# A two-layer graph network: ten and eight node tiles by counts instead of nine and seven, layer 2's first rows fetched in layer 1, and pools that wait for their own bytes

## The chip, the core and the metric

One core of one Trainium2 chip runs the whole program. The metric is the device time of one execution in microseconds (us), the median of several runs. The engines are TensorE (PE, matrix products; its weight loads are PEld), VectorE (DVE), ScalarE (ACT), GpSimd (POOL) and SyncE (SP, which only issues DMAs). Each engine runs its own instructions in the order in which they were written.

## The reference

6250 nodes have 256 features each, and 100,000 edges are sorted by `dst`. `dst` is the integer part of 6250 u² for uniform u, so nodes with low numbers receive many more edges than the others. All is fp32.

```
agg = segment_sum(x[src], dst); h = (1+eps1)*x + agg
h = relu(h @ W1a + b1a)          # 256 -> 512
h = relu(h @ W1b + b1b)          # 512 -> 512
agg = segment_sum(h[src], dst); h = (1+eps2)*h + agg
h = relu(h @ W2a + b2a)          # 512 -> 512
out = h @ W2b + b2b              # 512 -> 256
return layernorm(x + out)
```

## The kernel before

The nodes are 49 tiles of 128 (the last has 106 rows). A layer aggregates each tile in one of two ways, and then runs its dense part.

**By gathers.** POOL issues an indirect DMA (line 503) that fetches 128 source rows of the table into a piece of a ring (`early`; in layer 2 also `late`). PE sums the 128 rows into up to 32 nodes with a one-hot matrix (L1177, `bank<-early,sel`, two fp32 matmuls a gather in the trace), a split and merge (ACT L1207, DVE L1212, PE L1222) places the sums, and DVE adds them to the tile's `acc` (L1234). A gather can be issued when a piece of the ring is free, that is, when PE has summed what was in it.

**By counts.** For the "heavy" tiles, those with the lowest numbers and so the most edges, the kernel makes a matrix that says how many edges lead from each source node to each node of the tile. It is counted in layer 1 by products of one-hot factors (PE L1886, `bank<-cb,ca`, factors by DVE L1833 and L1843; ACT L1927 and DVE L1935 copy the counts into `at` and `at_first`). Counts times table then replace the gathers:

- Layer 1 (L1761, `bank<-cf,xh`) takes the heavy tiles in three passes of `PASSED` tiles each. Every pass runs over the 49 row tiles of x, in two fp32r halves kept in DRAM (`halves`), so a matmul is as wide as its pass has tiles times 128 columns: 256, 512 and 384.
- Layer 2 (L1613, `bank<-upper,cf` and `bank<-xr,cf`) runs over 13 ranges of the 49 row tiles, the last range (one tile) first, then ranges of four tiles. For a range, SP loads the rows of h (`xr<-h`, L866) and the saved counts (`ci<-counts`, L1527), ACT and DVE split the rows in two halves (L1503, L1504, L1508), ACT converts the counts (L1540, `cf<-ci`), and for each heavy tile PE multiplies 2 x 4 matmuls into a bank, which ACT (L1551) or DVE (L1556) adds to `acc`.

The number of heavy tiles is `HEAVY` = (9, 7): nine in layer 1, seven in layer 2. All others are gathered: 454 gathers in layer 1, 494 in layer 2 (rows of 512 fp32, twice as long).

The dense part of a tile transposes `acc` (PE L1300, ACT L1321), and multiplies twice (PE L1349, ACT L1359 with relu, PE L1378). In layer 1, DVE L1388 and ACT L1391 finish the tile, and ACT's queue writes it to h (`h<-h1r`, L866). In layer 2, DVE L1400 to L1423 and ACT L1418 make the layernorm. Layer 2's gathers may read any row of h, so its first one waits for layer 1's last write of h.

**What sets the order.** A planner simulates the engines with a cost for each operation when the program is built. Each step is a `yield ("on", engine, cost, priority)`; of the steps that are ready, an engine takes the one with the lowest number. The order that comes out is fixed in the program. Where PE has nothing ready, `filling()` inserts matmuls without a use (L1246, `bank<-numbers`, priority 9). Buffers come from pools `keep`, `loan` and `psum`, opened anew for each layer.

Of the kernel before, what the change touches and what calls it, by code (L numbers as in the profile page):

```python
# [26 lines left out]
HEAVY = (9, 7)  # L27
# [4 lines left out]
RANGE = 4  # L32
PAIR = 2
PASSED = (2, 4, 3)
# [178 lines left out]
def dve(n):  # L213
    return 0.085 + 0.00105 * n


def act(n):
    return 0.12 + 0.00083 * n
# [152 lines left out]
def tile_gin_residual_layernorm(  # L371
# [520 lines left out]
    def ordered(ctx):  # L892
# [20 lines left out]
        halves = odram.tile([N, 2 * D], F32, name="halves")  # L913

        def layer(number, ctx, table, width, scale, wa, ba, wb, bias, wide):
# [17 lines left out]
            class Tiles(Room):  # L933

                def __init__(self, pool, shape, dtype, name, bufs):
                    super().__init__(plan, bufs, False)
                    self.make = lambda: pool.tile(shape, dtype, tag=name, name=name, bufs=bufs)

# [33 lines left out]
            ready = {t: Event(plan) for t in range(NT)}  # L972

# [63 lines left out]
            def scaling(b, token):  # L1037
# [8 lines left out]
                yield ("on", "ACT", act(len(ts) * width), 2)  # L1046
# [208 lines left out]
            def dense(b):  # L1255
# [115 lines left out]
                for i, t in enumerate(ts):  # L1371
# [11 lines left out]
                    def finish(token=token, i=i, t=t, m=m, po=po, todo=todo):  # L1383
                        if once:
# [7 lines left out]
                            in_parts(nc.scalar, h1[t * P : t * P + m, :], h[:m])  # L1392
                            h_token.release()
# [71 lines left out]
            cf_room = Tiles(loan, [P, max(PASSED) * P] if once else [P, RANGE, P], F32R, "cf", 3)  # L1465
# [4 lines left out]
            def second_products():  # L1470
                xr_room = Tiles(loan, [P, RANGE, width], F32R, "xr", 2)
                upper_room = Tiles(loan, [P, RANGE, width], F32R, "upper", 2)
                ci_rooms = [
                    Tiles(
                        loan, [P, RANGE, len(ts) * P], U8 if ts[0] else U16, f"ci{ts[0]}", 2
                    )
                    for ts in kept
                ]
# [8 lines left out]
                def rows_of():  # L1487
                    for r in rs:
# [6 lines left out]
                        upper = upper_token.tile  # L1495
                        halves_of[r] = xr_token, upper_token
                        whole = xr.bitcast(F32)
                        todo = Count(plan)
                        for j, k in enumerate(ks):
                            m = rows(k)  # L1500
                            token = yield ("get", banks, 2)
                            yield ("on", "ACT", 2 * act(width), 3)
                            nc.scalar.copy(upper[:m, j, :], whole[:m, j, :])  # L1503
                            nc.scalar.copy(bank[token.number][:m, :width], whole[:m, j, :])  # L1504

                            def lower(j=j, m=m, token=token):
                                yield ("on", "DVE", dve(width), 3)
                                nc.vector.tensor_tensor(  # L1508
                                    xr[:m, j, :], bank[token.number][:m, :width], upper[:m, j, :],
                                    op=ALU.subtract,  # L1510
                                )
                                token.release()
                                todo.less()

                            todo.more()
                            plan.then(plan.start, lower())
                        yield ("until", todo)
# [117 lines left out]
            def first_products():  # L1635
# [62 lines left out]
                def factoring():  # L1698
                    for n, ts in enumerate(PASSES):
# [9 lines left out]
                        for k in range(NT):  # L1709
# [12 lines left out]
                            if k + 1 in ends:  # L1722
                                plan.start(saving(ts, ranges[ends.index(k + 1)]))
# [517 lines left out]
```

## Time and profile before

| | us |
|---|---|
| median of 3 runs (lowest, highest) | 1544.63 (1540.19, 1547.57) |
| profiled execution | 1555.75 |
| its span from the first to the last instruction | 1553.9 |
| PE busy (share of the span) | 1296.1 (83%) |
| POOL busy | 919.0 (59%) |
| DVE busy | 801.4 (52%) |
| ACT busy | 599.3 (39%) |

The profile is one execution, 11 us longer than the median. Stages, by the names of instructions: until 27 us the lists of edges are prepared, layer 1 runs to its last write of h at about 760 us, the first gather of layer 2 stands at 765.25 and its last at 1514.92. A busy time counts an instruction from start to end; neighbouring matmuls overlap, so the mean duration of a matmul is above the spacing of a dense run of them.

### The profile page before, as it was taken

The numbers are of one execution on the slowest core, as the hardware profiler recorded it, in microseconds if no ns is written. First come the engines' busy times: TensorE is split into PE (matmuls) and PEld (weight loads), VectorE is DVE, ScalarE is ACT, GpSimd is POOL, SyncE is SP. The second block draws the span as 40 slices with busy tenths as digits, with TensorE's granted clock in tenths as the row PEclk, the third lists the DMA queues.
The fourth block names the chain that finished last, engine by engine and source line by source line (L and its number), as shares of the span: only waits on it lengthen the run. The fifth ranks groups of instructions, "written<-read, shape, count | busy, mean of one in ns | idle before, by whom it ended". The sixth has DMA issues, their size and how long they took to land.

```text
span 1553.9 us, 20355 instructions
## 1 busy us (share of the span) xinstructions
PE 1296.1 (83%) x6363; PEld 806.0 (52%) x6363; DVE 801.4 (52%) x2078; ACT 599.3 (39%) x1256; POOL 919.0 (59%) x976
## 2 busy tenths in 40 slices
PE   3478888887888889998878898998989799899866
PEld 2144454444544446654435566665656566566533
DVE  5575666666457762122146666765555454433331
ACT  3655665544554434432433433423332333211111
POOL 7556665556656665663265666665666566566560
PEclk7589999988989999999999999999999999999988
DMA  4554776645865337962588677777787677666661
GB/s 119 160 172 139 234 227 192 219 131 157 252 207 176 113 116 230 293 182 81 175 284 299 206 242 224 263 219 238 240 252 227 214 241 243 186 199 192 190 205 28
DMA packets 156749, 309.63 MB, mean 199 GB/s; under 512 B 35118, under 2 KB 69894, under 8 KB 156632
## 3 DMA queue, kind: packets, MB, share of 16 engines
q0 software_dynamic: 61312, 189.07, 40.3%
q1 hardware_dynamic: 87844, 105.57, 21.0%
q10 hardware_dynamic: 7476, 13.60, 2.4%
q8 instruction: 54, 0.88, 0.2%
q14 instruction: 63, 0.52, 0.1%
HBM read 269.32 MB, written 38.82 MB: 198 GB/s over the span
## 4 chain that ended last, share of the span: by engine, by line
PE 63%; DVE 11%; issue 9%; another core or an unknown queue 7%; ACT 4%; DMA 2%; DVEq 0%; SPq 0%; ACTq 0%
PE bank L1349 16%; PE bank L1378 14%; PE bank L1177 10%; PE bank L1613 7%; PE bank L1761 7%; PE bank L1886 4%; PE bank L1222 3%; DVE acc L1234 3%; PE bank L1300 2%; DMA acc<-h 1%; DVE at L1935 1%; DVE acc L1556 1%; PE bank L1246 1%; DVE split L1212 1%
## 5 line engine op out<-in xcount | busy, mean ns | idle before, releaser
L503 POOL DMA_INDIRECT early<-in_x_dram,srcs x454 | 442.4, 974 | 271.6 <-issue 114.6
L503 POOL DMA_INDIRECT early<-h,srcs x250 | 241.0, 964 | 190.2 <-issue 113.1
L503 POOL DMA_INDIRECT late<-h,srcs x244 | 233.2, 956 | 134.5 <-issue 62.9
L1234 DVE SCALAR_TENSOR_TENSOR acc<-bank,mask,acc 128x256 f32<-128x256 f32 (+1 forms) x369 | 211.6, 611 | 73.4 <-PE bank L1222 27.5
L1177 PE MATMUL bank<-early,sel 128*32 128x256 f32 (+1 forms) x1408 | 166.8, 502 | 42.6 <-issue 24.0
L1378 PE MATMUL bank<-wide_w,ht 128*128 128x512 f32 (+1 forms) x392 | 195.6, 626 | 6.4 <-DVE h1r L1388 3.2
L1349 PE MATMUL bank<-zt,wide_w 128*128 128x256 f32 (+2 forms) x832 | 184.0, 375 | 18.6 <-issue 11.1
L1349 PEld LDWEIGHTS bank<-zt,wide_w 128*128 128x128 f32 x832 | 152.4, 194 | 50.6 <-issue 19.2
L1761 PE MATMUL bank<-cf,xh 128*128 128x256 f32 (+3 forms) x588 | 142.6, 376 | 23.1 <-issue 14.4
L1613 PE MATMUL bank<-upper,cf 128*128 128x512 f32 (+1 forms) x343 | 151.6, 442 | 8.1 <-ACT upper L1503 4.3
L1927 ACT CAST at<-bank 128x441 f32 (+4 forms) x214 | 106.1, 507 | 95.7 <-PE bank L1886 25.7
L1613 PE MATMUL bank<-xr,cf 128*128 128x512 f32 (+1 forms) x343 | 137.9, 402 | 3.0 <-issue 1.3
L1126 DVE TENSOR_TENSOR sel<-iota,slot 128x256 f32<-128x256 f32 (+4 forms) x111 | 48.8, 440 | 164.4 <-PE bank L1177 94.5
L1886 PE MATMUL bank<-cb,ca 128*128 128x490 f16 (+7 forms) x347 | 89.7, 349 | 52.3 <-DVE cb L1843 21.1
L1761 PEld LDWEIGHTS bank<-cf,xh 128*128 128x128 f32 (+1 forms) x588 | 101.0, 198 | 56.1 <-issue 34.3
L1556 DVE TENSOR_TENSOR acc<-bank,acc 128x512 f32<-128x512 f32 x84 | 56.9, 684 | 129.0 <-remote 69.5
L1222 PE MATMUL bank<-split,to 128*128 128x512 f32 (+2 forms) x310 | 90.6, 399 | 39.1 <-ACT split L1207 17.3
L1540 ACT CAST cf<-ci 128x512 fp32r<-128x512 uint8 (+3 forms) x91 | 53.3, 594 | 175.6 <-remote 56.6
L1177 PEld LDWEIGHTS bank<-early,sel 128*32 128x32 f32 x1408 | 40.1, 112 | 148.1 <-issue 124.9
L1349 PE MATMUL bank<-zt,narrow_w 128*128 128x256 f32 (+2 forms) x432 | 105.4, 394 | 11.7 <-ACT zt L1321 8.2
L1843 DVE TENSOR_SCALAR cb<-numbers,spot 128x492 f16<-128x492 f16 (+7 forms) x328 | 94.7, 327 | 36.2 <-PE bank L1886 12.9
L1378 PEld LDWEIGHTS bank<-wide_w,ht 128*128 128x128 f32 (+1 forms) x392 | 73.1, 198 | 77.5 <-issue 64.4
(150 smaller groups left out, 1702.3 us busy)
## 6 DMA issues: line engine op xcount, KB each, us to landing
xh<-halves SPq DMA_DIRECT2D x48, 512.0 KB
h<-h1r ACTq DMA_DIRECT2D x48, 256.0 KB
halves<-xh SPq DMA_DIRECT2D x24, 512.0 KB
xr<-h SPq DMA_DIRECT2D x12, 1024.0 KB
acc<-h SPq DMA_DIRECT2D x19, 512.0 KB
early<-in_x_dram,srcs POOLq DMA_INDIRECT x454
raw<-in_x_dram SPq DMA_DIRECT2D x12, 512.0 KB
r<-in_x_dram SPq DMA_DIRECT2D x22, 256.0 KB
```

Of the source, the lines that this page charges most:

```text
L503: nc.gpsimd.indirect_dma_start(out=rows_[:, j, :], out_offset=None, in_=table, in_offset=bass.IndirectOffsetOnAxis(ap=srcs[:, c : c + 1], ...
L1177: mm = nc.tensor.matmul(pm[b * SLOTS : (b + 1) * SLOTS], sel[:, c - groups[g][0], :], rows_[:, l, :], start=(c == part[0]), stop=(c == par ...
L1222: nc.tensor.matmul(pu[:, i * width : (i + 1) * width], to[:used], split[:used, l, i * width : (i + 1) * width], start=(l == 0), stop=(l == 1),
L1234: nc.vector.scalar_tensor_tensor(acc[t], pu[:, i * width : (i + 1) * width], mask[:, t - lo[g], g : g + 1], acc[t], op0=ALU.mult, op1=ALU.add,
L1349: nc.tensor.matmul(ph[:, (f - o) * TILES * P : (f - o) * TILES * P + nb], wa[:, k, f * P : (f + 1) * P], zt[:, k, :nb], start=(k == 0), st ...
L1378: nc.tensor.matmul(po[:m], ht[:, f, i * P : i * P + m], wb[:, f, :], start=(f == 0), stop=(f == KH - 1),)
L1556: nc.vector.tensor_tensor(acc[t], bank[token.number][:, :width], acc[t], op=ALU.add)
L1613: nc.tensor.matmul(bank[token.number][:, :width], cf[:m, j, :], of[:m, j, :], start=(j == 0 and of is upper), stop=(j == len(ks) - 1 and o ...
L1761: nc.tensor.matmul(to[:, :c], of, factor, start=(k == 0 and l == 0), stop=last, skip_group_check=True,)
L1843: made = nc.vector.tensor_scalar(token.tile[:, :e], numbers[:, :e], spot[:, c : c + 1], None, op0=ALU.is_equal,)
L1886: mm = nc.tensor.matmul(bank[token[l].number][:, : (k1 - k0) * w], a.tile[:, c % BATCH, :], b.tile[:, k0 * w : k1 * w], start=(j == 0), st ...
L1927: nc.scalar.copy(of[:, k0:k1, UNDER - w + 1 :][:, :, bass.ds(v, w - 1)], ap[:, :, : w - 1],)
```

## The change

- `HEAVY` (9, 7) becomes (10, 8) and `PASSED` (2, 4, 3) becomes (2, 4, 4): one more tile by counts in each layer.
- `SOONER` = 2: a new task `sooner()` in layer 1 waits until all counts are saved and the rows of h in question are written, then loads the first two ranges of layer 2 (one tile and four tiles) and halves them with `halving()`, at priority 8, the lowest of real work.
- `at` and `at_first` move into a pool of their own, which is closed in layer 1; the bytes go to a pool `side2` with the buffers `xr`, `upper`, `cfs` and `ci` of layer 2, given out there by the class `Views`.
- The pools `keep`, `loan`, `psum` and `side2` get `reuse_waits="tile"`: a buffer waits for the former users of its own bytes only.
- The counting matmuls go from priority 1 to 0 on PE. The scaling of `acc` on ACT in layer 2 goes from priority 2 to 4.

```diff
-HEAVY = (9, 7)
+HEAVY = (10, 8)
...
+SOONER = 2
 PAIR = 2
-PASSED = (2, 4, 3)
+PASSED = (2, 4, 4)
...
+        def make_views():
+
+            side.close()
+            pool = ctx.enter_context(tc.tile_pool(name="side2", bufs=1, side="right", reuse_waits="tile"))
...
+            some("xr", 2, [RANGE, H], F32R)
+            some("upper", 2, [RANGE, H], F32R)
+            some("cfs", 3, [RANGE, P], F32R)
+            for ts in kept:
+                some(f"ci{ts[0]}_", 2, [RANGE, len(ts) * P], U8 if ts[0] else U16)
...
-            keep = ctx.enter_context(tc.tile_pool(name=f"keep{number}", bufs=1))
-            loan = ctx.enter_context(tc.tile_pool(name=f"loan{number}", bufs=1))
+            keep = ctx.enter_context(tc.tile_pool(name=f"keep{number}", bufs=1, reuse_waits="tile"))
+            loan = ctx.enter_context(tc.tile_pool(name=f"loan{number}", bufs=1, reuse_waits="tile"))
             psum = ctx.enter_context(
-                tc.tile_pool(name=f"psum{number}", bufs=1, space=bass.MemoryType.PSUM)
+                tc.tile_pool(name=f"psum{number}", bufs=1, space=bass.MemoryType.PSUM, reuse_waits="tile")
             )
...
-                yield ("on", "ACT", act(len(ts) * width), 2)
+                yield ("on", "ACT", act(len(ts) * width), 2 if once else 4)
...
+            def halving(ks, xr, upper, width, first, todo):
+
+                whole = xr.bitcast(F32)
+                for j, k in enumerate(ks):
+                    m = rows(k)
+                    token = yield ("get", banks, first - 1)
+                    yield ("on", "ACT", 2 * act(width), first)
+                    nc.scalar.copy(upper[:m, j, :], whole[:m, j, :])
+                    nc.scalar.copy(bank[token.number][:m, :width], whole[:m, j, :])
+
+                    def lower(j=j, m=m, token=token):
+                        yield ("on", "DVE", dve(width), first)
+                        nc.vector.tensor_tensor(
+                            xr[:m, j, :], bank[token.number][:m, :width], upper[:m, j, :],
+                            op=ALU.subtract,
+                        )
+                        token.release()
+                        todo.less()
...
-                    for r in rs:
+                    for i, r in enumerate(rs):
                         ks = ranges[r]
                         xr_token = yield ("get", xr_room, 0)
                         xr = xr_token.tile
-                        in_rows(ks, xr.bitcast(F32), table)
-                        yield ("rest", LOAD + 3.0)
+                        if i >= SOONER:
+                            in_rows(ks, xr.bitcast(F32), table)
+                            yield ("rest", LOAD + 3.0)
...
+                def sooner():
+                    yield ("until", saved)
+                    make_views()
+                    for i, r in enumerate(reversed(range(len(ranges) - SOONER, len(ranges)))):
+                        ks = ranges[r]
+                        for k in ks:
+                            yield ("until", written[k])
+                        xr = views["xr"][i]
+                        in_rows(ks, xr.bitcast(F32), h1[:, :])
+                        yield ("rest", LOAD + 3.0)
+                        yield from halving(ks, xr, views["upper"][i], H, 8, Count(plan))
...
-                        yield ("on", "PE", sum(0.01 + NT * wides[x[1]] / 2400 for x in todo[k : k + 2]), 1)
+                        yield ("on", "PE", sum(0.01 + NT * wides[x[1]] / 2400 for x in todo[k : k + 2]), 0)
```

Lines below the edits move by 34 or so: L1177 before is L1211 in the changed kernel, L1613 is L1648, L1503 and L1504 are L1509 and L1510, L1391 is L1425.

On ACT, the last writes of layer 1 and the first range of layer 2 stood like this before (`h1r` is a finished tile of layer 1, `upper` the upper half of a range's rows, `cf` the converted counts):

```order
L1391 ACTIVATE h1r<-h1r 128x512
L866 DMA h_60<-h1r 128x512
L1047 ACTIVATE acc<-acc,e_93 128x1024 x4
L1540 CAST cf<-ci_7010 128x128
L1503 CAST upper<-xr 106x512
L1504 COPY bank_6972<-xr 106x512
```

In the changed kernel the halving stands among the finishing of layer 1's tiles, at this place on ACT:

```order
L1355 COPY zt<-bank_498 128x2x128
L1509 CAST upper_6770<-xr_6768 128x512
L1510 COPY bank_501<-xr_6768 128x512
L1425 ACTIVATE h1r<-h1r 128x512
L867 DMA h_60<-h1r 128x512
L1509 CAST upper_6770<-xr_6768 128x512
L1510 COPY bank_502<-xr_6768 128x512
L1425 ACTIVATE h1r<-h1r 128x512
L867 DMA h_60<-h1r 128x512
```

All five row tiles of the first two ranges are halved there, and ACT's layer 2 starts with conversions of counts.

On PE, the first sums of gathered rows of layer 2 stood before in the midst of the second range, here ahead of its fourth heavy tile (24 of its 56 matmuls are ahead of the sums):

```order
L1613 MATMUL bank_6972<-upper,cf 128x512
L1613 MATMUL bank_6972<-xr,cf 128x512
L1177 MATMUL bank_6974<-early,sel_7034 32x512 x2
L1177 MATMUL bank_6975<-early,sel_7034 32x512 x4
L1177 MATMUL bank_6976<-early,sel_7043 32x512 x4
L1613 MATMUL bank_6977<-upper,cf 128x512
```

In the changed kernel they stand behind all products of both ranges, and what follows (`upper_6769`) is the third range:

```order
L1648 MATMUL bank_7133<-upper_6770,cfs_6771 128x512
L1648 MATMUL bank_7133<-xr_6768,cfs_6771 128x512
L1211 MATMUL bank_7128<-early,sel_7180 32x512 x2
L1211 MATMUL bank_7134<-early,sel_7180 32x512 x4
L1211 MATMUL bank_7129<-early,sel_7193 32x512 x4
L1648 MATMUL bank_7130<-upper_6769,cfs_6772 128x512
```

So 80 product matmuls (16 of the one-tile range, 64 of the next) are ahead of the first sum, where 38 were.

Near the end of PE's order, the last product of layer 2 before had 100 of the 494 gathers' sums behind it:

```order
L1613 MATMUL bank_6972<-upper,cf 128x512
L1613 MATMUL bank_6972<-xr,cf 128x512
L1177 MATMUL bank_6974<-late,sel 32x512 x12
L1300 MATMUL bank_6973<-ident,acc 128x128 x4
L1300 MATMUL bank_6976<-ident,acc 128x128 x4
```

In the changed kernel the last product stands among the last tiles' dense parts:

```order
L1648 MATMUL bank_7129<-upper_6769,cfs_6772 128x512
L1648 MATMUL bank_7129<-xr_6767,cfs_6772 128x512
L1256 MATMUL bank_7133<-split,to 128x512 x2
L1383 MATMUL bank_7130<-zt,wide_w 128x128 x8
L1334 MATMUL bank_7134<-ident,acc 128x128 x4
L1383 MATMUL bank_7128<-zt,wide_w 128x128 x8
L1211 MATMUL bank_7132<-early,sel 32x512 x8
```

Of 474 sums 20 are left behind it. By counts of the orders, the changed kernel has 442 and 474 gathers (12 and 20 fewer), 98 more products in layer 2, 24 more counting matmuls, 196 products of layer 1 with 512 instead of 384 columns, and 42 matmuls of L1246 instead of 98. Behind layer 1's last sum PE has 16 first and 8 second dense matmuls before, and 32 and 20 in the changed kernel (the trace shows each of these fp32 matmuls as two).

## Rows read from the trace of the kernel before

**Rows 1.** The page: busy time of each engine, share of the span, instructions.

```profile
PE 1296.1 (83%) x6363; PEld 806.0 (52%) x6363; DVE 801.4 (52%) x2078; ACT 599.3 (39%) x1256; POOL 919.0 (59%) x976
```

**Rows 2.** Windows by stage: from:to, length, each engine's busy us, clock, DMA share, GB/s.

```profile
120.00:720.00 600.00, 508.05 (x2572) 299.13 (x2565) 327.66 (x901) 286.88 (x639) 370.94 (x381) 0.93 0.61 189
720.00:760.00 40.00, 37.52 (x172) 19.93 (x171) 6.79 (x13) 10.03 (x25) 0.00 (x0) 0.96 0.28 87
760.00:800.00 40.00, 27.68 (x89) 12.93 (x87) 9.08 (x18) 19.92 (x40) 23.39 (x25) 0.83 0.79 276
800.00:1470.00 670.00, 600.39 (x2937) 407.33 (x2936) 363.34 (x721) 212.62 (x415) 421.81 (x440) 0.98 0.73 229
1470.00:1554.00 84.00, 57.58 (x307) 31.73 (x305) 22.41 (x55) 10.23 (x25) 28.94 (x31) 0.85 0.41 120
```

**Rows 3.** Windows of POOL's gathers (L503) alone: busy us and number, clock, DMA.

```profile
27.00:720.00 693.00, 425.66 (x438) 0.89 0.60 185
765.00:1516.00 751.00, 474.14 (x494) 0.96 0.73 230
```

**Rows 4.** Waits of POOL, 120 to 720 us: releaser, us in total, times, longest.

```profile
POOL early L503 <- PE bank L1177: 47.3, 20, 5.3
POOL early L503 <- PE bank L1886: 45.0, 22, 5.3
```

**Rows 5.** Waits of POOL, 800 to 1480 us.

```profile
POOL late L503 <- PE bank L1177: 44.2, 11, 10.4
POOL early L503 <- PE bank L1177: 32.5, 7, 7.3
```

**Rows 6.** Groups of PE by shape: count, busy us, mean ns, idle before.

```profile
L1761 PE MATMUL bank<-cf,xh 128*128 128x512 f32 x192 | 59.6, 442 | 14.4 <-issue 10.7 <-ACT cf L1719 3.7
L1761 PE MATMUL bank<-cf,xh 128*128 128x384 f32 x192 | 46.9, 374 | 6.3 <-ACT cf L1719 4.6 <-issue 1.7
L1886 PE MATMUL bank<-cb,ca 128*128 128x275 f16 x19 | 7.2, 383 | 18.5 <-DVE cb L1843 15.5 <-DVE at L1935 1.7 <-DVE acc L1234 1.2
```

**Rows 7.** Pieces of the chain that ended last: start us, us, what.

```profile
514.66 0.60 PE bank L1886 x4
...
1231.14 1.85 PE bank L1613 x8
...
1456.78 2.71 PE bank L1177 x24
```

**Rows 8.** Windows of PE's L1246 alone (clock and DMA are the stage's).

```profile
705.00:760.00 55.00, 7.03 (x21) 1.96 (x22) 0.94 0.31 97
760.00:800.00 40.00, 7.96 (x27) 2.45 (x24) 0.83 0.79 276
1470.00:1554.00 84.00, 15.55 (x48) 4.42 (x48) 0.85 0.41 120
```

**Rows 9.** Timeline of PE at layer 1's end, behind its last sum.

```profile
747.94 3.84 PE L1349 MATMUL bank<-zt,narrow_w 128*128 128x128 f32 x32
751.61 7.03 PE L1378 MATMUL bank<-wide_w,ht 128*128 128x512 f32 x16
```

**Rows 10.** Timeline at layer 2's start: start us, us, instruction, [idle before <-releaser].

```profile
765.60 0.80 PE L1613 MATMUL bank<-upper,cf 106*128 106x512 f32 x1 [4.34 <-ACT upper L1503]
...
778.11 0.50 PE L1613 MATMUL bank<-upper,cf 128*128 128x512 f32 x1 [2.05 <-issue]
...
783.89 0.63 PE L1613 MATMUL bank<-xr,cf 128*128 128x512 f32 x1
784.32 0.61 PE L1613 MATMUL bank<-upper,cf 128*128 128x512 f32 x1
```

**Rows 11.** The chain at layer 2's end.

```profile
1504.30 14.39 another core or an unknown queue
1518.70 0.59 ACT split L1207
...
1538.67 0.67 PE bank L1300 x4
```

More of the change, by code (lines that the diff above doesn't have):

```diff
@@ L913, in ordered, with some @@
         halves = odram.tile([N, 2 * D], F32, name="halves")
+        side = ExitStack()
+        sides = side.enter_context(tc.tile_pool(name="side1", bufs=1, side="right"))
+        at = sides.tile([P, NT, -(-(HEAVY[0] * P + UNDER - BASE) // 4) * 4], U8, name="at")
+        at_first = sides.tile([P, NT, P + UNDER + UNDER % 2], U16, name="at_first")
+        views = {}
+        def make_views():
+            side.close()
+            pool = ctx.enter_context(tc.tile_pool(name="side2", bufs=1, side="right", reuse_waits="tile"))
+            def some(name, count, shape, dtype):
+                views[name] = [
+                    pool.tile([P] + shape, dtype, name=f"{name}{i}") for i in range(count)
+                ]
+            some("xr", 2, [RANGE, H], F32R)
[3 more added lines that the diff above has]
+                some(f"ci{ts[0]}_", 2, [RANGE, len(ts) * P], U8 if ts[0] else U16)
         def layer(number, ctx, table, width, scale, wa, ba, wb, bias, wide):
@@ L937, in __init__, with take @@
                     self.make = lambda: pool.tile(shape, dtype, tag=name, name=name, bufs=bufs)
+            class Views(Room):
+                def __init__(self, views):
+                    super().__init__(plan, len(views), False)
+                    self.views = views
+                def take(self):
+                    token = super().take()
+                    token.tile = self.views[token.number]
+                    return token
             def reach(g):
@@ L972, in layer @@
             ready = {t: Event(plan) for t in range(NT)}
+            written = {t: Event(plan) for t in range(NT)}
             def settle(t):
@@ L1392, in finish @@
                             in_parts(nc.scalar, h1[t * P : t * P + m, :], h[:m])
+                            plan.then(written[t].set)
                             h_token.release()
@@ L1463, in beside_rows @@
                 return some
-            cf_room = Tiles(loan, [P, max(PASSED) * P] if once else [P, RANGE, P], F32R, "cf", 3)
+            cf_room = Tiles(loan, [P, max(PASSED) * P], F32R, "cf", 3) if once else Views(views["cfs"])
+            def halving(ks, xr, upper, width, first, todo):
[14 more added lines that the diff above has]
+                        todo.less()
+                    todo.more()
+                    plan.then(plan.start, lower())
             if once:
@@ L1491, in rows_of @@
                         xr = xr_token.tile
-                        in_rows(ks, xr.bitcast(F32), table)
-                        yield ("rest", LOAD + 3.0)
+                        if i >= SOONER:
+                            in_rows(ks, xr.bitcast(F32), table)
+                            yield ("rest", LOAD + 3.0)
                         upper_token = yield ("get", upper_room, 0)
-                        upper = upper_token.tile
                         halves_of[r] = xr_token, upper_token
[L1497 to L1517, printed above, removed]
+                        if i >= SOONER:
+                            todo = Count(plan)
+                            yield from halving(ks, xr, upper_token.tile, width, 3, todo)
+                            yield ("until", todo)
                         plan.then(halved[r].set)
@@ L1736, in saving @@
                             )
+                    saved.less()
                 def multiplying():
```

15 lines of the change are left out of this document (5 added, 10 removed).

## The prediction

> **What bounds the kernel now.** I read the page's busy times first, then the windows by stage, because a share over the whole span mixes stages with different limits. PE is the busiest engine, 1296.1 us of 1553.9, and POOL is far from full [rows 1]. By stage, PE is busy 508 of 600 us in layer 1's main part (density 0.847) and 600 of 670 in layer 2's (0.896), POOL only 371 and 422 [rows 2]. The gathers, on which POOL spends 0.96 us each, follow each other at a slower pace: 693 us for 438 is 1.58 us in layer 1, 751 us for 494 is 1.52 in layer 2 [rows 3]. So POOL itself doesn't set the pace. What it waits for is PE: in layer 1, 47.3 us end with sums and 45.0 with counting matmuls [rows 4] (POOL's idle time there is 600 - 371 = 229 us), in layer 2, 76.7 us with sums [rows 5]. POOL waits for a free piece of the ring, the piece waits for its sum, and the sum waits for its turn in PE's fixed order. Neither PE nor the gathers bound alone: PE's order holds the gathers back, and gathers not yet landed leave PE idle.
>
> Three stretches are worse than this steady state:
> - The end of layer 1 (720 to 760): POOL does nothing, since layer 2's gathers need all of h; PE is busy 37.5 of 40 us, but from 705 on 7.0 us of that are matmuls of L1246, which do nothing useful [rows 2, 8].
> - The start of layer 2 (760 to 800): PE is busy 27.7 us, 8.0 of them L1246, so 20.3 us of 40 are lost [rows 2, 8]. Its first product waited 4.34 us for ACT to halve rows, and the second range came 12.5 us later, after another gap [rows 10].
> - The end of layer 2 (1470 to 1554): of 84 us PE is busy 57.6, and 15.6 of these are L1246, so 42 us are lost [rows 2, 8]. The products are over by then, and the chain stands 14.4 us on something in flight before the last merge [rows 11]; the last gather was issued at 1514.92.
>
> **Layer 1, part by part.** PE gets more work. The 196 matmuls of the third pass become 512 wide: the 384-wide ones take 374 ns and the 512-wide ones 442, 68 ns more, so at most 13.3 us; by the spacing in a dense run, a matmul of 512 takes 1.85/8 = 0.23 us [rows 7], a quarter of it 0.058, so 11.3 [rows 6]. I take 12. The 24 counting matmuls cost 24 x 0.15 = 3.6 us in a dense run [rows 7] and 24 x 0.383 = 9.2 at their full duration [rows 6]; I take 6. The eight more of the small products with the identity and two merges fewer are about nothing, within 1 us either way. Twelve gathers fewer save PE about 2 us: half as wide as layer 2's, whose sums take 2.71/12 = 0.226 us a gather [rows 7], they cost between half of that and all of it, 1.4 to 2.7. Sum: +16 us of PE. The copies of the counts on ACT and DVE (24 each) lie beside: ACT is busy 287 and DVE 328 of 600 us [rows 2]; if that cover were gone, they would add their own durations, by the nearest row 24 x 0.38 = 9 us [rows 6].
>
> The gathers get shorter: 12 x 1.58 = 19 us. But more dense work is behind the last sum: 64 and 40 matmuls of the trace instead of 32 and 16, so at 3.84/32 and 7.03/16 us each [rows 9] 25.3 us instead of 10.9, +14. With a few us of L1246 and waits that stood in this tail replaced, I take +11. So if gathers lead, layer 1 changes by -19 + 11 = -8. If PE leads, it is +16, less about 10 us for the L1246 matmuls and gaps of the end that the dense work now fills: +6. If nothing is filled it is +16. The rows speak for both: of POOL's 229 us idle 92 are for PE [rows 4], the rest are not. I take the middle of the first two, **-1 us**, and keep -8 and +16 as bounds. Moving the counting to priority 0 on PE is in this: it frees counts earlier and makes sums wait; 45 us of POOL's waits already end with counting matmuls [rows 4], so it can cost as well as gain, and I give it no term.
>
> **Layer 2's start.** The first two ranges are halved during layer 1. On ACT and DVE that is ten copies and five subtractions in a stretch where both are mostly idle (10.0 and 6.8 of 40 us) [rows 2], ahead of some of the last writes of h; there it could delay the first gather by the copies that stand in front of the last write, one pair or two, which the range holds. At the start PE then has 80 products ready as soon as counts are there, 42 more than stood ahead of the first sum before. At 0.23 us they are 9.7 us of work in a stretch where 20 us were lost. The sums behind them don't come later for it, since their rows had not landed by then. I take **-8 us**; bounds 0 (the counts land too late as well, or the first landings decide) and -12 (the whole gap to the second range).
>
> **Layer 2's middle.** 98 products more x 0.23 = +22.6 us, 20 gathers' sums fewer x 2.71/12 = 0.226 are -4.5 [rows 7], two merges fewer -1: +17 us of PE. At the stage's density of 0.896 that is 17/0.896 = **+19 us**. The other bound is the gathers' side, 20 x 1.52 = -30 us.
>
> **Layer 2's end.** Products now reach almost to the last sum (20 sums behind the last product instead of 100), so the 42 us lost at the end have work to fill them. The last tile's way from its last gathered row to the output can't be filled: from 1538.67, where the last transpose starts [rows 11], it is 15.2 us to the end of the span. That leaves 42 - 15 = **-27 us** at best for PE; lower bound -10, where only the matmuls of L1246 are replaced in part and the wait for the last landings stays.
>
> **The sum.** -1 - 8 + 19 - 27 = -17 us. Against the profiled execution of 1555.75 this gives about 1539, and since that execution lies 11 us above the median, 1544.63 - 17, about **1527 us** by the median. That pools wait for their own bytes alone and the scaling of `acc` has gone to priority 4 is costed at nothing beside this: before, ACT's scalings stood ahead of the first halving, which is now in layer 1; the start's bounds hold it.
>
> **Clock.** PE's granted clock shows in the rows: 0.83 in 760 to 800 and 0.85 in the last 84 us, against 0.98 in the middle [rows 2]; two neighbouring products at the start are 0.43 us apart [rows 10], against 0.23 in the dense run. So after idle time PE runs at the lower of its two levels, 1.2 GHz, for a while. The change leaves out 56 of 98 matmuls of L1246. The Trainium skill ("TensorE: Matmul & The Clock Gate", section "HAM oscillation — how this bites in real kernels") says that PE which waits for data falls back to the cold clock and starts the next burst cold, which speaks against leaving them out. The trace agrees that the clock is lower where PE waits.
>
> **Rivals.**
> - *PE is the bound and the end doesn't give back* (slower). The end's gap may belong to the last gathers' landing, not to the order [rows 11], and PE at 0.896 may take no more. Then layer 1 costs +16, the middle +19, the start gives -8, the end -10: +17, about 1562 us. For it: 33 us of PE added and the longest wait at the end has POOL's last gathers in it. Against: the end's 100 sums without a product beside them. It decides where the last product still comes long before the end, or density in the middle stays under 0.90.
> - *Gathers set the pace throughout* (much faster). Layer 1 -8, start -8, middle and end -30, the tail as before: -46, about 1499 us. For it: the constant pace [rows 3]. Against: POOL's waits end with PE [rows 4, 5], and PE has more to do.
> - *Nothing comes of the fetch in layer 1, and gains and work cancel*: the start 0 because the saved counts and the first gathers' landing decide as before, layer 1 +2, middle +19, end -20: +1, about 1545.
> - *The clock falls* where L1246 is missing: the start and the end at 0.5 instead of 0.84 would take 28 + 42 us of work 0.84/0.5 = 1.7 times as long, at most +47; as products take the place of most L1246 matmuls, I price it at +18 on the forecast, again 1545.
>
> **Chances.** Forecast 0.45 (its own range 1515 to 1537), PE as the bound 0.24, gathers as the pace 0.16, cancelling 0.10, clock 0.05. A measurement of this kernel can tell about 0.5%, 8 us, from no change: faster (under 1537) 0.45 + 0.16 = 0.61, same 0.15, slower 0.24. The range reaches from 1497 (half of the gather case is left out, 0.08) to 1560 (half of the PE case, 0.12).
>
> **What would show it.** Right: in the 40 us after layer 1's last write PE has over 34 us of useful work; the stretch from layer 1's last sum to its last write grows to some 25 us, and that write comes at 759 +- 10; products run to within 40 us of the end, the L1246 matmuls there are few, and the lost time of the last 84 us is under 20. Wrong: layer 1's last write after 770 (counting at priority 0 starves the sums, POOL's waits on L1886's successor grow), a gap of PE in the first 40 us of layer 2 as long as before (counts not there), gathers at 1.6 us and more in layer 2, or the same wait of 14 us before the last merge.

## The result, and the profile after

The changed kernel takes 1526.76 us (median of 4 runs, 1519.56 to 1538.76); the kernel before, run beside it, 1546.1 us. The ratio is 0.989, with a 95% interval from 0.9847 to 0.9934: faster, by about 1.1%. 1527 us were predicted. The profiled execution took 1526.32 us with a span of 1524.6; that of before took 1555.75 us, 10 us above its median, so the two profiles differ by 29 us where the medians differ by 19. Below, differences between the two profiles are told as such.

Windows of the changed kernel by stage, with the columns of [rows 2]; its layer 1 ends at 745.52, so the stages are shifted:

```profile
690.00:745.00 55.00, 54.66 (x243) 29.57 (x241) 14.96 (x27) 19.31 (x47) 4.17 (x5) 1.00 0.28 98
...
745.00:785.00 40.00, 25.83 (x102) 16.58 (x106) 8.58 (x17) 20.09 (x40) 20.88 (x22) 0.87 0.65 210
...
785.00:1441.00 656.00, 591.00 (x2844) 399.43 (x2837) 359.83 (x710) 209.65 (x403) 413.92 (x429) 0.96 0.73 230
1441.00:1525.00 84.00, 71.75 (x398) 54.19 (x396) 28.02 (x69) 15.40 (x39) 22.07 (x24) 0.93 0.37 113
```

Windows of the filler matmuls alone (L1246 before, L1280 now), to be held against [rows 8]:

```profile
745.00:785.00 40.00, 6.18 (x17) 1.53 (x17) 0.87 0.65 210
785.00:1441.00 656.00, 0.76 (x2) 0.19 (x2) 0.96 0.73 230
1441.00:1525.00 84.00, 3.29 (x10) 1.03 (x10) 0.93 0.37 113
```

Take the fillers from PE's busy time. In the last 84 us PE did 42.0 us of useful work before and does 68.5 now: the end of layer 2 is filled. The last 55 us of layer 1 are full at clock 1.00. In the first 40 us of layer 2 this measure shows no gain: 27.7 - 8.0 = 19.7 us before [rows 2, 8] and 25.8 - 6.2 = 19.6 now. But the work behind these busy times is not the same. Windows of the products of layer 2 alone in the first 40 us behind the last write of h (L1613 before, L1648 now):

```profile
760.00:800.00 40.00, 16.90 (x42) 9.78 (x43) 0.83 0.79 276
...
745.50:785.50 40.00, 23.91 (x80) 15.79 (x80) 0.87 0.65 207
```

And of the sums of gathered rows (L1177 before, L1211 now):

```profile
760.00:800.00 40.00, 7.16 (x20) 1.62 (x20) 0.83 0.79 276
...
745.50:785.50 40.00, 0.96 (x12) 0.36 (x16) 0.87 0.65 207
```

PE did 80 products instead of 42, and 12 matmuls of sums instead of 20. At their spacing in a dense run [rows 7] that is 38 x 0.23 - 8 x 0.11, an estimated 8 us of work more, in the same busy time. After 60 us both have done 44 matmuls of sums, with 121 products now and 81 before.

Layer 2's gathers, as in [rows 3], and then three places of the timeline of the changed kernel: POOL at layer 1's last gather, ACT at its last write, POOL at layer 2's first and last gather.

```profile
748.00:1485.00 737.00, 456.87 (x474) 0.96 0.72 227
```

```profile
694.44 0.94 POOL L504 DMA_INDIRECT early<-in_x_dram,srcs  x1 [0.31 <-issue]
...
745.52 0.33 ACTq L867 DMA_DIRECT2D h<-h1r  x1
...
748.48 0.95 POOL L504 DMA_INDIRECT early<-h,srcs  x1 [53.09 <-PE bank L1648]
...
1477.62 0.95 POOL L504 DMA_INDIRECT late<-h,srcs  x1 [0.31 <-issue]
```

The same four instants in the trace of the kernel before:

```profile
716.12 0.95 POOL L503 DMA_INDIRECT early<-in_x_dram,srcs  x1 [0.30 <-issue]
...
760.07 0.33 ACTq L866 DMA_DIRECT2D h<-h1r  x1
...
765.25 0.95 POOL L503 DMA_INDIRECT early<-h,srcs  x1 [48.19 <-issue]
...
1514.92 0.95 POOL L503 DMA_INDIRECT late<-h,srcs  x1 [0.30 <-issue]
```

And PE's last sums of gathered rows in layer 1, eight matmuls, before and now:

```profile
743.68 0.64 PE L1177 MATMUL bank<-early,sel 128*32 128x256 f32 x8
...
717.58 0.64 PE L1211 MATMUL bank<-early,sel 128*32 128x256 f32 x8
```

From these the 29 us of the profiles can be laid out. Layer 1's last gather is 21.7 us earlier, its last sums are 26.1 us earlier, and its last write 14.6 us. From the last gather to the last write it takes 51.1 us instead of 44.0; from the last sums to it, where only dense work is left, 27.9 instead of 16.4. Layer 2 from that write to the end of the span takes 793.8 us before and 779.1 now, 14.7 less. Its gathers last 729.1 us instead of 749.7, 1.54 each instead of 1.52, and behind the last one there are 47 us instead of 39.

### The profile page after: what moved, and what is told of

It reads as the page before. It is cut to its first block, busy times and chain, and to the rows that moved or that the text cites. A ratio compares the mean times of both kernels' runs of the same rounds, so it can differ in the third digit from the quotient of the medians.

```text
span 1524.6 us, 20531 instructions
## 1 busy us (share of the span) xinstructions
PE 1297.8 (85%) x6367; PEld 820.3 (54%) x6367; DVE 811.6 (53%) x2122; ACT 618.4 (41%) x1293; POOL 895.2 (59%) x944
## 4 chain that ended last, share of the span: by engine, by line
PE 69%; DVE 9%; issue 8%; another core or an unknown queue 4%; ACT 4%; DMA 2%; POOL 1%; DVEq 1%; ACTq 1%; SPq 0%; POOLq 0%
PE bank L1383 17%; PE bank L1412 15%; PE bank L1211 11%; PE bank L1648 9%; PE bank L1811 7%; PE bank L1936 4%; PE bank L1256 4%; PE bank L1334 2%; DVE at L1985 1%; DVE cb L1893 1%; DVE acc L1591 1%; DVE acc L1268 1%; DMA xh<-halves 1%; DVE sel L1160 1%
## 5 line engine op out<-in xcount | busy, mean ns | idle before, releaser
L504 POOL DMA_INDIRECT early<-h,srcs x238 | 229.7, 965 | 186.5 <-issue 61.5
L1268 DVE SCALAR_TENSOR_TENSOR acc<-bank,mask,acc 128x512 f32<-128x512 f32 (+1 forms) x365 | 210.9, 611 | 80.0 <-PE bank L1256 21.4
L1211 PE MATMUL bank<-early,sel 128*32 128x256 f32 (+1 forms) x1360 | 157.4, 489 | 30.2 <-issue 20.3
L1648 PE MATMUL bank<-upper,cfs 128*128 128x512 f32 (+1 forms) x392 | 169.4, 432 | 14.6 <-issue 10.9
L1811 PE MATMUL bank<-cf,xh 128*128 128x512 f32 (+2 forms) x588 | 150.2, 389 | 17.1 <-ACT cf L1752 10.2
L1648 PE MATMUL bank<-xr,cfs 128*128 128x512 f32 (+1 forms) x392 | 155.5, 397 | 0.0
L1977 ACT CAST at<-bank 128x250 f32 (+4 forms) x238 | 113.9, 494 | 99.7 <-PE bank L1936 32.6
L1575 ACT CAST cfs<-ci 128x512 fp32r<-128x512 uint8 (+3 forms) x104 | 60.7, 595 | 220.8 <-PE bank L1648 80.1
L1160 DVE TENSOR_TENSOR sel<-iota,slot 128x256 f32<-128x256 f32 (+3 forms) x109 | 47.6, 436 | 164.8 <-PE bank L1211 122.2
L1256 PE MATMUL bank<-split,to 128*128 128x512 f32 (+3 forms) x306 | 89.8, 398 | 38.7 <-DVE split L1246 19.4
L1211 PEld LDWEIGHTS bank<-early,sel 128*32 128x32 f32 x1360 | 40.0, 112 | 127.0 <-issue 107.0
```

The costliest lines, as they stand in the source:

```text
L504: nc.gpsimd.indirect_dma_start(out=rows_[:, j, :], out_offset=None, in_=table, in_offset=bass.IndirectOffsetOnAxis(ap=srcs[:, c : c + 1], ...
L1211: mm = nc.tensor.matmul(pm[b * SLOTS : (b + 1) * SLOTS], sel[:, c - groups[g][0], :], rows_[:, l, :], start=(c == part[0]), stop=(c == par ...
L1256: nc.tensor.matmul(pu[:, i * width : (i + 1) * width], to[:used], split[:used, l, i * width : (i + 1) * width], start=(l == 0), stop=(l == 1),
L1268: nc.vector.scalar_tensor_tensor(acc[t], pu[:, i * width : (i + 1) * width], mask[:, t - lo[g], g : g + 1], acc[t], op0=ALU.mult, op1=ALU.add,
L1648: nc.tensor.matmul(bank[token.number][:, :width], cf[:m, j, :], of[:m, j, :], start=(j == 0 and of is upper), stop=(j == len(ks) - 1 and o ...
L1811: nc.tensor.matmul(to[:, :c], of, factor, start=(k == 0 and l == 0), stop=last, skip_group_check=True,)
```

## The experiments

The kernels ran in three sets of four, each on a chip of its own. Chips differ: on that of the first set the kernel before takes 1584 us, on those of the second and the third 1284 each. Only ratios to the kernel before on the same chip are compared.

### First set: the change taken apart (before: 1583.59 us)

**The changed kernel again**, as a control.

> The changed kernel as it is, timed beside its parts on one chip. Both theories: about 1527 us, 0.985 to 0.993 of the kernel before; layer 1's last write of h near 745 us (760 before), layer 2 from there some 779 us (794 before).

Measured: 1563.06 us, ratio 0.9877 (0.9817 to 0.9937). The ratio is the same as in the first comparison.

**The counts alone.**

```diff
 (the kernel before)
-HEAVY = (9, 7)
+HEAVY = (10, 8)
-PASSED = (2, 4, 3)
+PASSED = (2, 4, 4)
```

> The kernel before with HEAVY (10, 8) and PASSED (2, 4, 4) alone: no earlier halving, pools and priorities as before. Theory (the sum of the prediction: one tile more by counts in each layer pays by fewer gathers and by a filled end of layer 2): -1 + 19 - 27 = -9 us, about 1536, and the lost time of the last 84 us falls under 25. Rival (the counts cost PE what they save in gathers, and the earlier halving and the counting priority made the gain): 1540 to 1550, layer 1's last write no earlier than 757.

Measured: 1591.9 us, ratio 1.0081 (1.0046 to 1.0116), slower by 0.8%. The theory falls: one tile more by counts does not pay by itself. The rival's range missed too.

**All but the counts.**

```diff
 (the changed kernel)
-HEAVY = (10, 8)
+HEAVY = (9, 7)
-PASSED = (2, 4, 4)
+PASSED = (2, 4, 3)
```

> The changed kernel with HEAVY (9, 7) and PASSED (2, 4, 3): all but the tile more by counts. Theory: only the start's -8 us is left, about 1537, and the end of layer 2 keeps its 42 us lost. Rival (halving, pools and priority made the gain): about 1527, layer 1's last write near 745.

Measured: 1587.29 us, ratio 1.0026 (0.9987 to 1.0065). No gain: neither the start's -8 us of the theory nor the rival's whole gain is there.

**Counting back to priority 1.**

```diff
 (the changed kernel)
-                        yield ("on", "PE", sum(0.01 + NT * wides[x[1]] / 2400 for x in todo[k : k + 2]), 0)
+                        yield ("on", "PE", sum(0.01 + NT * wides[x[1]] / 2400 for x in todo[k : k + 2]), 1)
```

> The changed kernel with counting matmuls at priority 1 on PE again. Theory (no term for it): within 5 us of the changed kernel, 1522 to 1532, layer 1's last write at 740 to 750. Rival (counting ahead of products is what made layer 1 some 14 us shorter, where the prediction had 1 us): about 1540, layer 1's last write near 757.

Measured: 1582.8 us, ratio 0.999 (0.9953 to 1.0027). The whole gain is gone with one digit; the rival holds, with even more than it said.

So on this chip the gain needs the counts and their priority together; the change without either gives nothing. (Whether these two alone are enough was not run on this chip.) Where the gain goes, the timelines show: POOL's last gather of layer 1 and ACT's last write of h. With the counts alone:

```profile
709.06 0.95 POOL L503 DMA_INDIRECT early<-in_x_dram,srcs  x1 [0.30 <-issue]
...
775.96 0.33 ACTq L866 DMA_DIRECT2D h<-h1r  x1
```

With all but the priority:

```profile
705.16 0.95 POOL L504 DMA_INDIRECT early<-in_x_dram,srcs  x1 [0.30 <-issue]
...
773.61 0.33 ACTq L867 DMA_DIRECT2D h<-h1r  x1
```

And in the changed kernel, on the same chip:

```profile
701.66 0.94 POOL L504 DMA_INDIRECT early<-in_x_dram,srcs  x1 [0.30 <-issue]
...
753.68 0.33 ACTq L867 DMA_DIRECT2D h<-h1r  x1
```

The reader sees 66.9 and 68.5 us from the last gather to the last write at priority 1, and 52.0 at priority 0; the last gather itself moves by 3.5 us between the last two. PE's work behind the last gather says why. In the groups of PE's instructions in that stretch, here with priority 1 (from 705 us), products of counts are still to be done, and more second dense matmuls:

```profile
L1412 PE MATMUL bank<-wide_w,ht 128*128 128x512 f32 x88 | 40.3, 595 | 0.0
...
L1811 PE MATMUL bank<-cf,xh 128*128 128x512 f32 (+1 forms) x36 | 9.9, 415 | 0.0
```

In the changed kernel there are no products left (from 702 us):

```profile
L1412 PE MATMUL bank<-wide_w,ht 128*128 128x512 f32 x76 | 34.8, 598 | 0.0
```

The order of PE agrees: the last product stands after 434 of 442 gathers' sums with priority 1 (also with the counts alone) and after 406 with priority 0; the last counting matmul after 366 and 342. A third pass of four tiles cannot begin before its counts are complete, and what is late in it, and the dense parts of its four tiles, is work behind the last gather, where POOL has nothing to do until all of h is written. With nine tiles and priority 0 the last product stands after 386 of 454 sums, which is earlier than before the change (402), but the work behind the last sum is the same 16 and 8 matmuls: nothing to win. The two profiles that differ by the priority alone are 25 us apart, the medians 20; their granted clocks, 0.919 and 0.943, are apart too, while over all fast runs these two kernels have 0.919 to 0.947 and 0.923 to 0.955, so part of the 25 us is not the priority's.

Last gather and last write with all but the counts:

```profile
718.81 0.95 POOL L504 DMA_INDIRECT early<-in_x_dram,srcs  x1 [0.30 <-issue]
...
764.33 0.33 ACTq L867 DMA_DIRECT2D h<-h1r  x1
```

This write comes 10.7 us later than in the changed kernel, but 9 to 12 us earlier than with the counts at priority 1. Layer 2, from the last write to the end of the span, shows the opposite: 823.4 us with all but the counts, 803.6 with the counts alone, 811.4 with all but the priority, 806.4 in the changed kernel. The windows of the last 84 us say why, PE in all and the fillers alone, first for the counts alone, then for all but the counts:

```profile
1495.60:1579.60 84.00, 73.47 (x416) 54.29 (x414) 31.30 (x80) 17.27 (x44) 19.34 (x20) 0.98 0.30 92
1495.60:1579.60 84.00, 4.53 (x14) 1.37 (x14) 0.98 0.30 92
...
1503.70:1587.70 84.00, 53.06 (x275) 31.38 (x275) 17.04 (x38) 9.64 (x23) 26.87 (x29) 0.78 0.35 104
1503.70:1587.70 84.00, 13.52 (x43) 3.95 (x43) 0.78 0.35 104
```

Useful work is 68.9 us with the counts alone and 39.5 without them. So the counts fill the end of layer 2 by themselves, as the theory of the first experiment said; what they win there they lose in layer 1, unless counting goes first. (Each is one execution; that of the counts alone was 10.5 us below its median.)

### Second set: fetch, pools, and a further step (before: 1284.05 us)

**No fetch in layer 1.**

```diff
 (the changed kernel)
-SOONER = 2
+SOONER = 0
```

> The changed kernel with SOONER = 0: no rows of layer 2 fetched or halved in layer 1. Theory now (counts pay when counting goes first on PE; the fetch in layer 1 only moves the start's gap to where the counts land): the same as the changed kernel, a ratio of 0.984 to 0.992 to the kernel before. Rival (the prediction's start term of -8 us): 0.993 or more, and a gap of PE in the first 40 us of layer 2 that is some 8 us longer than the changed kernel's.

Measured: 1283.79 us, ratio 1.0003 (0.998 to 1.0025), no gain over the kernel before.

**Pools without waits by tile.** `, reuse_waits="tile"` is taken out in all four places.

> The changed kernel without reuse_waits on its four pools. Theory: the same as the changed kernel, 0.984 to 0.992. Rival (the pools' waits are what lets layer 2 start early): 0.994 or more, with the first gather or the first product of layer 2 over 5 us later behind layer 1's last write.

Measured: 1287.75 us, ratio 1.0021 (0.9998 to 1.0045).

**Counts and priority alone.** The kernel before with the diff of the counts alone, and the counting matmuls at priority 0.

> The kernel before with two parts alone: HEAVY (10, 8) with PASSED (2, 4, 4), and counting matmuls at priority 0. Theory: these two are the whole gain, 0.984 to 0.992, with layer 1's last write at most 56 us behind its last gather (67 us with the counts alone). Rival (the fetch and the pools carry half of it): 0.993 to 1.000.

Measured: 1296.78 us, ratio 1.0074 (1.0045 to 1.0103), slower by 0.7%. The layer-1 part of the theory holds (52.6 us from the last gather to the last write), the ratio does not.

**Counts fetched in layer 1 as well.**

```diff
 (the changed kernel)
                         in_rows(ks, xr.bitcast(F32), h1[:, :])
+                        for ts, of in zip(kept, counts):
+                            nc.sync.dma_start(
+                                views[f"ci{ts[0]}_"][i][:, : len(ks), :], of[:, ks[0] : ks[0] + len(ks), :]
+                            )
...
-                            nc.sync.dma_start(ci[:, :n, :], of[:, ranges[r][0] : ranges[r][0] + n, :])
+                            if r < len(ranges) - SOONER:
+                                nc.sync.dma_start(ci[:, :n, :], of[:, ranges[r][0] : ranges[r][0] + n, :])
```

> The changed kernel, in which the fetch in layer 1 also loads the saved counts of the first two ranges. Theory (the gap of 10 us in the changed kernel's layer 2 ends when counts land): the gap in the second range goes, up to -6 us, a ratio 0.003 to 0.004 below the changed kernel's. Rival (the gap moves on to the third range's rows or the first gathered rows, which land no sooner): the same time as the changed kernel, 0.985 to 0.990.

Measured: 1286.17 us, ratio 1.0022 (0.9999 to 1.0045). The changed kernel was not run on this chip; on that of the third set, which is as fast, it has 1.0014 (below), and this one is no better. The question, what ends the gap of 10 us, is left open: on that chip PE's longest wait in the changed kernel's first 40 us of layer 2 is 4.5 us.

By their ratios, the kernels without the fetch and without waits by tile fell on their rivals' side, though neither shows the longer gap or the later start that its rival named; counts and priority alone lie above both ranges. None of the four was faster here. But the first set doesn't fit with that, since taking out one part after the other would then take away the whole 1.2% each time. The chip was the open point, so the next set has the changed kernel beside its parts.

### Third set: the same parts beside the changed kernel (before: 1283.93 us)

> The changed kernel once more, beside three kernels that each lack a part of it, since chips differ. Theory (the change trades gathers for PE work, so it pays where gathers land late and PE waits, and gives nothing where PE is full): a ratio of 0.985 to 0.993 where the kernel before takes over 1500 us, and 0.997 to 1.004 where it takes about 1285. Rival (the ratio doesn't depend on the chip, the earlier call of four was about the parts left out): 0.985 to 0.993 in either case.

The changed kernel measured 1287.05 us, ratio 1.0014 (0.9991 to 1.0037). The theory holds: on this chip the change itself is worth nothing.

> The changed kernel with SOONER = 0, beside the changed kernel. Theory: the fetch in layer 1 is worth under 0.2%, since the start's gap ends when counts and third rows land. Rival (the prediction's start term): 0.4% or more above the changed kernel.

Without the fetch: 1283.65 us, ratio 0.9989 (0.9967 to 1.0011). The rival, 0.4% above the changed kernel, is out; if anything the kernel without the fetch is the faster one, by 0.25%, which the intervals don't separate.

> The kernel before with the counts of (10, 8) and counting at priority 0, beside the changed kernel. Theory: it lacks the pools' shorter waits and ACT's later scaling, and is 0.3 to 0.7% above the changed kernel. Rival (counts and priority are the whole change): within 0.2% of it.

Counts and priority alone: 1291.74 us, ratio 1.0063 (1.0035 to 1.0091), by the medians 0.36% above the changed kernel, as the theory said. So the pools' waits, the fetch and ACT's later scaling together are worth about that. Without the fetch the other two are worth more: 1283.65 us against 1291.74, 0.6%, with intervals that do not overlap. On the faster chips, then, the counts with their priority cost 0.6 to 0.7%, and the rest of the change brings that back.

> The changed kernel without reuse_waits, beside the changed kernel. Theory: 0.2 to 0.5% above it, in layer 2's first 60 us. Rival (pools' waits are covered by the landing of rows): within 0.2% of it.

Without waits by tile: 1288.14 us, ratio 1.0029 (1.0004 to 1.0055), 0.1% above the changed kernel. The theory's 0.2 to 0.5% is not seen, and the two kernels can't be told apart.

Why does one chip show 1.2% and the other nothing? The page's first lines for the changed kernel on the faster chip:

```profile
PE 1206.1 (94%) x6367; PEld 790.5 (61%) x6367; DVE 808.7 (63%) x2122; ACT 626.2 (49%) x1293; POOL 894.1 (70%) x944
```

Its windows of layer 2's gathers alone, and of all engines in layer 2's main part:

```profile
635.00:1251.00 616.00, 455.23 (x474) 0.99 0.83 270
...
675.00:1200.00 525.00, 511.93 (x2726) 369.01 (x2725) 341.39 (x674) 208.28 (x388) 386.06 (x403) 0.99 0.83 270
```

The window of layer 2's main part on the slower chip of the first set:

```profile
793.00:1477.00 684.00, 597.65 (x2858) 402.37 (x2857) 360.77 (x713) 211.94 (x407) 410.57 (x427) 0.96 0.69 220
```

And POOL's waits in layer 2, first on the faster chip (650 to 1240 us), then on the slower one (780 to 1500 us):

```profile
POOL late L504 <- PE bank L1211: 16.7, 10, 7.4
...
POOL early L504 <- PE bank L1211: 4.2, 6, 1.3
```

```profile
POOL early L504 <- PE bank L1211: 67.1, 12, 14.1
POOL late L504 <- PE bank L1211: 66.8, 13, 14.6
```

The gathers go at 616/474 = 1.30 us here (1.54 on the chip of the first comparison), PE's density is 511.93/525 = 0.975 in layer 2 (597.65/684 = 0.874 on the slower chip), and POOL waits for PE's sums 21 us instead of 134. My reading: the change adds work to PE and takes gathers away. Where PE is full, the work is paid and the gathers were nearly free; where PE stands, waiting for what is in flight, it is the other way round. It fits the ratios, but it is not shown: the kernel before has no profile on a faster chip.

The start is seen in the first product's wait on the faster chip of the third set. For counts and priority alone, for the kernel without the fetch, and for the changed kernel:

```profile
638.53 0.79 PE L1613 MATMUL bank<-upper,cf 106*128 106x512 f32 x1 [4.29 <-ACT upper L1503]
```

```profile
629.51 0.50 PE L1648 MATMUL bank<-upper,cfs 106*128 106x512 f32 x1 [1.10 <-ACT upper L1509]
```

```profile
633.00 0.50 PE L1648 MATMUL bank<-upper,cfs 106*128 106x512 f32 x1 [1.51 <-ACT cfs L1575]
```

Without the fetch the wait is as short as with it. What it waited for stands on ACT and SP, in the kernel with counts and priority alone:

```profile
613.54 0.73 SPq L866 DMA_DIRECT2D xr<-h  x2
...
633.51 4.26 ACT L1047 ACTIVATE acc<-acc,e 128x1024 f32<-128x1024 f32 x4 [0.48 <-ACT h1r L1391]
...
637.87 0.61 ACT L1503 CAST upper<-xr 106x512 fp32r<-106x512 f32 x1
```

and without the fetch:

```profile
628.27 0.33 ACTq L867 DMA_DIRECT2D h<-h1r  x1
...
628.84 0.61 ACT L1509 CAST upper<-xr 106x512 fp32r<-106x512 f32 x1
```

The loads of the first rows were issued at 613.54, 20 us before ACT had finished layer 1's last tile; ACT then spent 4.26 us on four scalings of `acc` before it halved them. With the scalings at priority 4 it halves them 0.6 us after the last write. So this wait was made by ACT's order, and its 4.3 us are 0.33% of the time; that this is most of what the parts beside the counts are worth is likely, but no run changes ACT's priority alone.

## Why the prediction was right, point by point

**The time and the sign** were right: -17 us were forecast for the median, -19 measured. The terms behind it were not all right, and that the sum comes so close is in part luck: in the profiles layer 1 gave 13.6 us more than its term, the two profiles differ by 10 us more than the medians, and on the faster chips the same change is worth nothing, which the forecast has no condition for.

**Layer 1, -1 us (bounds -8 and +16): mis-sized.** In the profiles it is -14.6, outside the bounds. The tail was right: +11 us were forecast behind the last sum, and it grew by 11.5 (16.4 to 27.9; the same two numbers are found on the slower chip without and with the counts). What failed is the step before it, "I take the middle of the first two": the gathers led. They were to save 19 us, of which the middle left 12; the last sums came 26.1 us earlier. On the slower chip, with the counts against without them, it was 22.2 us at the last sums and 10.7 at the last write, so this is not only the long profiled execution of before. PE's 16 us more do not show as time. From 120 us to the last write, before and now:

```profile
120.00:760.00 640.00, 545.57 (x2742) 319.06 (x2735) 334.45 (x914) 296.91 (x664) 370.94 (x381) 0.93 0.59 183
...
120.00:745.50 625.50, 543.58 (x2721) 314.41 (x2719) 342.13 (x942) 310.72 (x684) 362.10 (x368) 0.96 0.61 188
```

PE is busy 2.0 us less in it and stands 12.5 us less, at a granted clock of 0.96 instead of 0.93. How the work divides between waits that it filled and the higher clock, and whether that clock belongs to the change or to this execution, is open.

**"I give it no term"**, of the counting's priority, failed outright as a reason. The forecast took the order as it stood, with 32 and 20 matmuls behind the last sum, and so held the priority's effect without knowing it: that is luck. At priority 1 the tail behind the last gather is 16 us longer and the gain is gone. It was not the freed counts against the starved sums, as the prediction weighed it, but the date of the last product.

**Layer 2's start, -8 us: the work came, the signs for it did not.** PE's useful time in the first 40 us is 19.6 us, as before, where over 34 were to show the term right. But in that time PE did 38 more products and 8 fewer matmuls of sums, an estimated 8 us of work (above): time without fillers was the wrong sign, since busy time is not work. A gap of the kind that was to show the term wrong is there too. Behind 56 of the 80 products PE stands for 10.32 us; the timeline of the changed kernel has this row:

```profile
776.00 0.80 PE L1648 MATMUL bank<-upper,cfs 128*128 128x512 f32 x1 [10.32 <-issue]
```

ACT and DVE start again within the same microsecond before, with waits of 12.0 us that the trace puts down to something remote. That counts landed late was my reading of it, and was not shown. The first product's wait of 4.34 us before [rows 10] was not for the halving itself but for four scalings ahead of it, 4.26 us on ACT as on the faster chip. What the fetch is worth in time on a slower chip no run shows alone. On the faster chips it could be left out at no loss.

**Layer 2's middle, +19 us, and end, -27 us: right.** PE's useful work of layer 2, the sum of the last three stages without fillers, grew from 685.65 - 24.27 = 661.4 [rows 2, 8] to 688.58 - 10.23 = 678.4 us, 17 us as worked out (the middle has 0.76 us of fillers in both). The last 84 us took 26.4 us more work, and the first set shows that this is the counts' doing. The wait of 14.4 us before the last merge [rows 11] is gone from the chain; the last product stands 52 us before the end, where within 40 was said, and the lost time of the last 84 us is 15.5 us, under the 20. Layer 2 in all took 14.7 us less, against 16 forecast; the middle's density hardly moved (599.6/670 = 0.895 before, 590.2/656 = 0.900 now, without fillers).

**The rivals.** *PE is the bound*: the sign in the first comparison and on the slower chip is against it. On the faster chip, where density in the middle is 0.975, the ratio is 1.0014, far from the 17 us more that the rival priced; the counts with their priority alone cost 8 to 10 us there by their ratios. *The gathers set the pace throughout* is half true for layer 1. In layer 2 20 gathers fewer shortened their stretch by 20.5 us, where that rival had 30. *Cancelling* is what the faster chips show in the total; its parts were not measured there. *The clock* did not fall: with 56 fillers fewer the mean granted clock is 0.935 instead of 0.926, and in the last 84 us 0.93 instead of 0.85 [rows 2], where PE has real work in their place. Around the stand of 10.32 us the clock fell, as these windows of the changed kernel show:

```profile
756.00:766.00 10.00, 8.61 (x37) 5.94 (x35) 1.38 (x2) 2.59 (x4) 7.60 (x8) 1.00 0.98 348
...
776.00:780.00 4.00, 4.00 (x9) 2.62 (x9) 0.40 (x2) 1.34 (x3) 0.00 (x0) 0.54 0.34 109
```

The Trainium skill ("TensorE: Matmul & The Clock Gate", section "HAM oscillation — how this bites in real kernels") says that PE which waits for data starts its next burst cold; the 0.54 behind this stand, whose cause is open, agrees.

What stays open: what ends the gap of 10 us at the start, what pools, fetch and ACT's priority are worth each, whether counts and priority alone give the gain on a slower chip, and why gathers follow each other faster on one chip than on another. No kernel was clearly faster than the kernel before on the faster chips: the best is within 0.1% of it.

## What to carry to other kernels

Trading transfers for matmuls paid here where the matmul engine waited, and not where it was full; before such a trade, read the density of the stage that pays and the waits that the transfers end, and measure on more than one chip, since both changed with it here. Compare what was done in a stage by counting instructions, not by busy time alone: here 20 us of busy time held 42 products before and 80 after. When a phase must end before the next may begin, look at what stands behind its last transfer: there a larger unit of work lengthens the tail, and the priority of the step that the unit waits for can decide the whole change. An earlier fetch is worth what the next wait leaves of it; here, on the first chip, another wait stood 20 us further on.

## What the runs showed of the hardware that was not expected

The kernel before took 1284 us on two chips and 1584 on a third, 1546 in the first comparison. With it went the pace of the gathers, for the changed kernel 616 us for 474 on the faster chip and 737 in the first comparison (both windows above). PE's busy time differs too, 1206 us against 1298 for one and the same program; the mean granted clocks of the two executions are 0.972 and 0.935, so part of it can be the clock, which was 0.54 behind a stand of 10 us in the one (above) and 0.99 in layer 2's main part in the other.
